# Layer 1: the last two chunks' weights summed on four column groups, with a DRAM trip of their own

## The chip, the cores and the metric

The kernel runs on one core of a Trainium2 chip. The metric is the device time of one execution in microseconds (us), lower is better. The engines are PE (matrix products), DVE (vector), ACT (scalar), POOL (GpSimd) and SP, which here only issues DMAs. Each engine takes its own instructions strictly in the order in which the program lists them.

## The reference, cut to what matters

Layer 0 is an attention block over 4096 positions with a gate; it is not touched. Layer 1 is what the change lies in:

```python
qkv = einsum('oc,bchw->bohw', w_qkv, x) + b_qkv        # b=2, 4 heads of 64, 4096 positions
attn = softmax(einsum('bhdn,bhdm->bhnm', q, k) * 64**-0.5, axis=-1)
out = einsum('bhnm,bhdm->bhdn', attn, v)
x = einsum('oc,bchw->bohw', w_out, out) + b_out + x
```

The sums of the softmax, that is the sum over m of the exponentials for each query n, are what the changed lines compute.

## The kernel before, in words

**Units and chunks.** Layer 1 works through 32 units, one for each image b, pair of heads g and block j of 512 queries. A unit goes over the 4096 keys in 32 chunks of 128, for both heads at once, so a chunk's weights are a tile `raw` of 128 keys x (2 heads x 512 queries), all in 32-bit floats. Sixteen chunks make a half n of a unit (NG = 2), and each half has its own maximum; `losts` holds the factor that puts the first half onto the second half's maximum.

**The pipeline.** One step t of the main loop handles a pair of chunks, and 16 steps make a unit. In step t the scores of pair t are made (PE, `score`, L888), their running maximum is taken (DVE, L905) and they are copied out of PSUM into the ring of raw tiles (ACT, L906, in `keep`). Eleven steps later (LAG = 11) the pair's maximum is added (DVE, `shift`, L977), the exponential is taken (ACT, `weigh`, L989), POOL adds the chunk to the sum of its half (L999 for the first two chunks of a half, L1001 for later ones), and PE multiplies it with the values (`gather`, L1030). The ring has 26 tiles, so the copy of chunk c + 26 (L906) can't start before all readers of chunk c, POOL's addition among them, are done. POOL also adds the shift to one chunk of each half itself (L966).

**Written order.** Every instruction keeps its program order on its engine (`seq`). Steps that don't belong to the pair at hand are hung on a step and a place by `at(t, place, ...)`. The places in a step are, in this order: scores, weights of an odd chunk, "start", "early", first chunk of the pair, "early end", second chunk, `gather`, "late", "late end", last shift, "end".

**The sums of a unit.** POOL doesn't add a unit's last two chunks (m = 30 and 31; L993 returns before). Instead, when `gather` reaches chunk 31 it takes the one PSUM bank of the pool `psm` (`misc`, one buffer, shared with keys, values, queries and transposes) and multiplies both chunks with a matrix of ones (L1043): four products of 32 output rows each, for two chunks and two heads, which go to PSUM rows 64 and 96. So two products write rows 64 to 95 and two write rows 96 to 127, and the second chunk is accumulated onto the first. One step later `total` (L1060) adds POOL's sums: four products for two halves and two heads, to rows 0, 32, 64 and 96; those of the second half are accumulated onto the chunks' sums. Another step later `keep_total` copies the bank to an SBUF tile `srow` (ACT, L1068; buffer "kv", two buffers, shared with the stores of keys and values), writes its four rows to DRAM (SP, L1073), reads them back turned, so that queries lie along partitions (SP, L1075), and takes the exponential for `losts`. Two steps later POOL's `add_sums` (L1151, L1152) joins the halves; then come `factors` (DVE L1158, POOL L1159) and `rows` (DVE L1169, POOL L1175 and L1178), which apply them to the outputs.

With t1 = t0 + 24 for a unit that starts at step t0, the chunks' products are at step t1 + 3 (which is step 11 of the next unit), `total` at t1 + 4, `keep_total` at t1 + 5, `add_sums` at t1 + 7. The last unit is summed in another way, so 31 units have these steps. In units 24 to 31 there is no work for later keys and values; they finish the first image's output instead, and POOL has two more additions there (L1206).

Of the kernel before, what the change touches and what calls it, by code (L numbers as in the profile page):

```python
# [8 lines left out]
F32 = mybir.dt.float32  # L9
AF = mybir.ActivationFunctionType  # L10
ALU = mybir.AluOpType
# [3 lines left out]
P = 128  # L15
NB = 512
# [4 lines left out]
D1 = 64  # L21
# [5 lines left out]
def conv_attention_kernel(  # L27
# [19 lines left out]
    nc = tc.nc  # L47
    B, _, N = x.shape
    NJ = N // NB
    NM = N // P  # L50
    PB = NB // P
# [156 lines left out]
    seq = tc.keep_in_program_order  # L208
# [3 lines left out]
    def at(t, place, step):  # L212
        extras.setdefault((t, place), []).append(step)
# [19 lines left out]
    with own0:  # L233
# [417 lines left out]
        def misc(name):  # L651
            return small_bank[0](name)
# [118 lines left out]
    with (  # L771
# [23 lines left out]
            (u, n): dram.tile([2, NB], F32, tag=f"neg_{u}_{n}", name=f"neg_{u[0]}{u[1]}{u[2]}_{n}")  # L795
            for u in units for n in range(NG)
        }
        sum1 = {
            u: dram.tile([NG * 2, NB], F32, tag="sum_{}_{}_{}".format(*u), name=f"sum_{u}")
            for u in units  # L800
        }
        first, begun, late = {}, set(), {}


# [217 lines left out]
        def gather(t):  # L1022
            u = b, g, j = units[t // NM]
            m = t % NM
            n = m // GS
            if m % GS == 0:
                avs1[u, n] = psv.tile([P, NB], F32, tag="av", name=f"av1_{b}_{g}_{j}_{n}")
            v = vs[b, g, m // PB]
            for k in range(2):
                seq(nc.tensor.matmul(  # L1030
                    avs1[u, n][k * D1 : (k + 1) * D1, :], v[:, m % PB, k, :], raws[t][:, k, :],
                    start=(m % GS == 0), stop=(m % GS == GS - 1),
                ))
            if on_tensor(t) and t % 2 == 1 and t != 2 * END - 1:
                late_sums((t - 1, t) if on_tensor(t - 1) else (None, t))
            elif t == 2 * END - 2:
                late_sums((t, t + 1))
            if m == NM - 1 and u != units[-1]:
                srows[u] = misc(f"sum1_{b}_{g}_{j}")
                for i in (t - 1, t):  # L1040
                    for k in range(2):
                        r = D1 * (NG - 1) + 32 * k
                        seq(nc.tensor.matmul(  # L1043
                            srows[u][r : r + 32, :], ones[:, :32], raws[i][:, k, :],
                            start=(i < t), stop=False, skip_group_check=True,
                        ))
            raws.pop(t - 2, None)
            if m % GS == GS - 1:
                a = l1.tile([P, NB], F32, tag="avs", name=f"avs1_{b}_{g}_{j}_{n}")
                seq(nc.scalar.copy(a, avs1.pop((u, n))))  # L1050
                avs1[u, n] = a

        def total(u):


            b, g, j = u
            for n in range(NG):
                for k in range(2):
                    r = D1 * n + 32 * k
                    seq(nc.tensor.matmul(  # L1060
                        srows[u][r : r + 32, :], ones[:, :32], accs[u, n][:, k, :],
                        start=(n < NG - 1), stop=True, skip_group_check=True,
                    ))

        def keep_total(u):
            b, g, j = u
            row = l1.tile([P, NB], F32, tag="kv", name=f"srow_{b}_{g}_{j}")
            seq(nc.scalar.copy(  # L1068
                row.rearrange("p (a m i) -> p a i m", m=P, i=2),
                srows[u].rearrange("p (a i m) -> p a i m", m=P, i=2),  # L1070
            ))
            for m in range(2 * NG):
                nc.sync.dma_start(out=sum1[u][m : m + 1, :], in_=row[32 * m : 32 * m + 1, :])  # L1073
            s = small.tile([P, NG, 2, PB], F32, tag="sums1", name=f"sums1_{b}_{g}_{j}")
            nc.sync.dma_start(  # L1075
                out=s.rearrange("p n k (a i) -> p (n k a) i", i=2),
                in_=sum1[u].rearrange("m (a p i) -> p (m a) i", p=P, i=2),
            )
            srows[u] = s
            seq(nc.scalar.activation(losts[u], losts[u], AF.Exp, scale=D1**-0.5))  # L1080

        def turned(a, name):
# [66 lines left out]
        def add_sums(u):  # L1149
            s, lost = srows[u], losts[u]  # L1150
            seq(nc.gpsimd.tensor_tensor(s[:, 0], s[:, 0], lost, ALU.mult))  # L1151
            seq(nc.gpsimd.tensor_tensor(s[:, 1], s[:, 1], s[:, 0], ALU.add))  # L1152

        def factors(u):
# [69 lines left out]
        for n, u in enumerate(units):  # L1224
            b, g, j = u
            t0 = n * US
            if n > 0:
                at(t0 - 9, "start", lambda u=u, b=b, j=j: fetch(("q", u), x1[b][j]))
                for q in range(4):
                    at(t0 - (3, 3, 2, 2)[q], "late", lambda u=u, q=q: next_queries(u, q))  # L1230
                at(t0 - 2, "start", lambda u=u: keep_next_queries(u, 0))
                at(t0 - 1, "start", lambda u=u: keep_next_queries(u, 1))
            if n < len(units) - NJ:
                to = (*units[n + NJ][:2], j)
                at(max(t0 - 1, 0), "start", lambda to=to: fetch(("kv", *to), x1[to[0]][to[2]]))
                for q in range(4):
                    at(t0 + 2 + q, "late", lambda to=to, q=q: next_keys(*to, q))
                    at(t0 + (6, 7, 9, 10)[q], "late", lambda to=to, q=q: next_values(*to, q))
                at(t0 + 6, "start", lambda to=to: store_keys(*to))
                for i, step in enumerate((t0 + 8, t0 + 11)):  # L1240
                    at(step, "start", lambda to=to, i=i: store_values(*to, i))

                t1 = (n // NJ * NJ + NJ - 1) * US
                at(t1 + 2 * j + 2, "start", lambda to=to: load_keys(*to))
                at(t1 + 2 * j + 3 + LAG, "start", lambda to=to: load_values(*to))
            for k in range(NG):
                t1 = t0 + (k + 1) * GS // 2
                places = ("early", "early" if (u, k) == (units[-1], NG - 1) else "late")
                for i, place in enumerate(places):
                    at(t1, place, lambda u=u, k=k, i=i: turn_max(u, k, i))  # L1250
                    at(t1, f"{place} end", lambda u=u, k=k, i=i: fold(u, k, i))
                at(t1 + 2, "end", lambda u=u, k=k: place_shift(u, k))
            t1 = t0 + US + GS // 2
            if u != units[-1]:
                at(t1 + 4, "late", lambda u=u: total(u))
                at(t1 + 5, "start", lambda u=u: keep_total(u))
                at(t1 + 1, "late", lambda u=u: lose(u))
                at(t1 + 7, "late end", lambda u=u: add_sums(u))
                at(t1 + 8, "end", lambda u=u: factors(u))
                for place, k in (("early", 1), ("late", 0)):  # L1260
                    at(t1 + 9, place, lambda u=u, k=k: turn_sums(u, k))
                    at(t1 + 9, f"{place} end", lambda u=u, k=k: rows(u, k))
            else:
                at(END + 1, "late", lambda u=u: last_lost(u))
                at(END + 4, "early", lambda u=u: late_sums((None, None)))
                at(END + 4, "early end", lambda u=u: keep_late(0))
                at(END + 5, "early", lambda u=u: turn_late(0))
                at(END + 5, "early end", lambda u=u: add_late(u, 0))
                at(END + 6, "early", lambda u=u: turn_sums(u, 0))
                at(END + 6, "early end", lambda u=u: first_rows(u))  # L1270
                at(END + LAG, "late", lambda u=u: turn_late(1))
                at(END + LAG, "late", lambda u=u: add_late(u, 1))
                at(END + LAG, "late", lambda u=u: turn_sums(u, 1))
                at(END + LAG, "late", lambda u=u: last_rows(u))
            if n >= len(units) - NJ:
                b0 = B - 2
                at(t0 - 1, "start", lambda b0=b0, j=j: fetch_output(b0, j))
                for o in range(CC):
                    for q in range(4):
                        step = t0 + ((2, 3, 4, 5), (6, 7, 9, 10))[o][q]  # L1280
                        at(step, "late", lambda b0=b0, j=j, o=o, q=q: project_out(b0, j, o, q))
                at(t0 + 6, "start", lambda b0=b0, j=j: output(b0, j, 0, 2))
                for part, step in enumerate((t0 + 8, t0 + 11)):
                    at(step, "start", lambda b0=b0, j=j, part=part: output(b0, j, 1, part))
# [172 lines left out]
```

## Time and profile before

| | |
|---|---|
| median of 3 runs | 4640.9 us (4640.56 to 4641.03) |
| the profiled execution's own time | 4640.95 us |
| its span, first to last instruction | 4639.2 us |
| layer 1, first scores | at 2057.8 us |
| one unit of layer 1 | 78.9 us (79.0 in the last eight) |
| mean granted TensorE clock | 0.996 |

The profile is of one execution. A row of a group of instructions reads: line of the kernel, engine, operation, result<-operands, how many; then busy time in all and the mean of one in ns; then idle time of the engine just before them and what ended most of it. A row of the timeline reads: start in us from the span's start, length in us, engine, line, operation; in brackets the engine's idle time before it and what ended it. A suffix "xN" in the timeline means that N instructions that followed closely are merged. Every fp32 matmul is recorded as two instructions. PEld is PE's loading of weights, which overlaps its products.

### The profile page before, as it was taken

How to read it: one execution, taken by the hardware profiler on the slowest of the kernel's cores; microseconds unless marked ns; L12 is line 12 of the kernel's file. 1: busy time of each engine (PE TensorE's matmuls, PEld its weight loads, DVE VectorE, ACT ScalarE, POOL GpSimd, SP SyncE). 2: the span in 40 equal slices, each digit the busy share in tenths (PEclk: the TensorE clock that was granted, in tenths of full speed). 3: DMA queues.
4: the chain of work that ended last, by engine and by line, in shares of the span. 5: the costliest groups of instructions: out<-in, count | busy, mean ns of one | idle time of the engine just before them, and what ended most of it. 6: DMA issues, size and time to landing. Idle time of an engine off the chain costs nothing. (4 is left out here: it accounts for less than half of the span.)

```text
span 4639.2 us, 73122 instructions
## 1 busy us (share of the span) xinstructions
PE 4499.0 (97%) x28490; PEld 1511.6 (33%) x28490; DVE 3833.4 (83%) x4443; ACT 3439.9 (74%) x4588; POOL 2514.8 (54%) x1307
## 2 busy tenths in 40 slices
PE   8999999999999999999999999999999999999998
PEld 3433333333333333333333333333333333323332
DVE  6777777777777777529999999999999999999997
ACT  3266666666666666668888888888888888888885
POOL 5300000000000000008999999999999999999995
PEclk9999999999999999999999999999999999999999
DMA  3100000000000000121111221111211112111213
GB/s 101 39 4 20 20 20 15 15 15 15 15 15 15 15 13 13 33 75 40 35 42 35 55 56 39 37 40 42 71 42 36 39 33 62 51 53 37 53 40 112
DMA packets 190475, 174.84 MB, mean 38 GB/s; under 512 B 120232, under 2 KB 121064, under 8 KB 190128
## 3 DMA queue, kind: packets, MB, share of 16 engines
q1 hardware_dynamic: 188272, 169.58, 13.2%
q8 instruction: 223, 3.65, 0.3%
q14 instruction: 124, 1.02, 0.1%
q10 hardware_dynamic: 1856, 0.59, 0.1%
HBM read 127.65 MB, written 42.48 MB: 37 GB/s over the span
## 5 line engine op out<-in xcount | busy, mean ns | idle before, releaser
L1001 POOL TENSOR_TENSOR acc<-acc,raw 128x1024 f32<-128x1024 f32 x821 | 1950.4, 2376 | 80.1 <-ACT raw L989 30.7
L402 DVE TENSOR_REDUCE mx<-a 128x1 f32<-128x512 f32 x2048 | 1315.5, 686 | 449.9 <-PE a L398 448.8
L439 ACT ACTIVATE p<-s 128x512 f32<-128x512 f32 x2048 | 1108.3, 595 | 702.5 <-PE a L398 367.6
L905 DVE TENSOR_TENSOR rmax<-s,rmax 128x1024 f32<-128x1024 f32 x960 | 1171.6, 1220 | 99.7 <-PE s L888 89.6
L436 PE MATMUL s<-q,kT 32*128 32x512 f32 x4096 | 1218.8, 640 | 0.0
L888 PE MATMUL s<-q,k 64*128 64x512 f32 x4096 | 1120.3, 637 | 98.1 <-ACT raw L906 93.2
L906 ACT COPY raw<-s 128x1024 f32<-128x1024 f32 x1024 | 1035.6, 1011 | 240.8 <-DVE rmax L905 163.5
L977 DVE TENSOR_TENSOR raw<-raw,shift 128x1024 f32<-128x1024 f32 x961 | 1160.7, 1212 | 3.3 <-ACT shift L959 1.8
L989 ACT ACTIVATE raw<-raw 128x1024 f32<-128x1024 f32 x1024 | 1084.9, 1060 | 62.8 <-DVE raw L977 27.7
L398 PE MATMUL a<-kT,q 32*128 32x512 f32 x4096 | 1129.8, 643 | 1.4 <-DVE mx L402 1.3
L1030 PE MATMUL av<-raw,v 128*64 128x512 f32 x4096 | 1007.4, 607 | 4.2 <-ACT raw L989 2.5
L451 PE MATMUL av<-p,v 128*32 128x256 f32 (+1 forms) x7904 | 650.1, 399 | 0.6 <-ACT avs L465 0.6
L501 POOL TENSOR_TENSOR f<-f,dyn 128x16 f32<-128x16 f32 x15 | 3.3, 221 | 1028.2 <-DVE f L500 1028.2
L888 PEld LDWEIGHTS s<-q,k 64*128 64x128 f32 x4096 | 316.8, 185 | 678.7 <-ACT raw L906 487.0
L436 PEld LDWEIGHTS s<-q,kT 32*128 32x128 f32 x4096 | 397.7, 183 | 426.3 <-issue 392.1
L1030 PEld LDWEIGHTS av<-raw,v 128*64 128x64 f32 x4096 | 242.4, 136 | 650.8 <-issue 476.4
L451 PEld LDWEIGHTS av<-p,v 128*32 128x32 f32 x7904 | 157.7, 108 | 751.5 <-issue 737.3
L552 POOL TENSOR_SCALAR res<-res 128x1024 f32<-128x1024 f32 x16 | 16.7, 1044 | 660.3 <-ACT res L551 660.3
L398 PEld LDWEIGHTS a<-kT,q 32*128 32x128 f32 x4096 | 305.2, 184 | 31.4 <-DVE mx L402 18.2
L999 POOL TENSOR_TENSOR acc<-raw,raw 128x1024 f32<-128x1024 f32 x64 | 152.1, 2376 | 60.9 <-ACT raw L989 60.3
L966 POOL TENSOR_TENSOR raw<-raw,row 128x1024 f32<-128x1024 f32 x63 | 151.7, 2407 | 37.9 <-DMA row<-neg 37.9
L935 DVE TENSOR_REDUCE negs<-rt 128x4 f32<-128x512 f32 x126 | 87.0, 690 | 58.8 <-PE rt L918 58.8
(338 smaller groups left out, 1913.5 us busy)
## 6 DMA issues: line engine op xcount, KB each, us to landing
row<-neg SPq DMA_DIRECT2D x64, 512.0 KB
x<-in_x_dram SPq DMA_DIRECT2D x16, 512.0 KB
res<-in_x_dram SPq DMA_DIRECT2D x16, 512.0 KB
x<-res SPq DMA_DIRECT2D x16, 512.0 KB
att<-rows SPq DMA_DIRECT2D x62, 128.0 KB
kd<-k1s SPq DMA_DIRECT2D x24, 256.0 KB
vd<-v1s SPq DMA_DIRECT2D x24, 256.0 KB
k<-kd SPq DMA_DIRECT2D x24, 256.0 KB
```

The costliest lines, as they stand in the source:

```text
L398: seq(nc.tensor.matmul(ps, qs0[u][r, bass.ts(i, P)], kTs[b][r, bass.ts(m, NB)], start=True, stop=True,))
L402: seq(nc.vector.tensor_reduce(mxs[u][:, i * H + h, m : m + 1], ps, AX.X, ALU.max))
L436: seq(nc.tensor.matmul(ps, kTs[b][r, bass.ts(m, P)], qs0[u][r, :], start=True, stop=True))
L439: seq(nc.scalar.activation(pt[:, k, :], ps, AF.Exp, scale=D0**-0.5))
L451: seq(nc.tensor.matmul(avs[u][32 * h : 32 * h + 32, cols], vs0[b][:, m, 32 * h : 32 * h + 32], pts[t, h // 2][:, h % 2, cols], start=(m == ...
L888: seq(nc.tensor.matmul(ps[:, k, :], ks[b, g, m // PB][r, bass.ts(m % PB, P)], qs1[u][r, :], start=True, stop=True,))
L905: seq(nc.vector.tensor_tensor(rmax[u, n], ps, before, ALU.max))
L906: seq(nc.scalar.copy(raw, ps))
L977: seq(nc.vector.tensor_tensor(raws[t], raws[t], shifts[u, t % NM // GS], ALU.add))
L989: seq(nc.scalar.activation(p, p, AF.Exp, scale=D1**-0.5))
L1001: seq(nc.gpsimd.tensor_tensor(accs[u, n], accs[u, n], p, ALU.add))
L1030: seq(nc.tensor.matmul(avs1[u, n][k * D1 : (k + 1) * D1, :], v[:, m % PB, k, :], raws[t][:, k, :], start=(m % GS == 0), stop=(m % GS == GS ...
```

## The change

The two last chunks' sums no longer share a PSUM bank with `total`. In `gather`, the four products write four different groups of 32 rows (32 columns of the PE array each) of a bank `csums`: rows 0 and 32 for chunk 30, rows 64 and 96 for chunk 31, nothing accumulated. A new step `keep_chunks`, hung on (t1 + 4, "start"), copies that bank to an SBUF tile (ACT), writes four rows to DRAM and reads them back turned (five DMAs on SP); `keep_total` does the same for `total` as before, through the common function `keep_rows`. `total` takes the `misc` bank anew and writes it with four products that accumulate nothing. `add_sums` adds the chunks' sums with two more additions of 128x8 on POOL.

```diff
             if m == NM - 1 and u != units[-1]:
-                srows[u] = misc(f"sum1_{b}_{g}_{j}")
-                for i in (t - 1, t):
+
+                csums[u] = misc(f"csum1_{b}_{g}_{j}")
+                for i in range(2):
                     for k in range(2):
-                        r = D1 * (NG - 1) + 32 * k
+                        r = D1 * i + 32 * k
                         seq(nc.tensor.matmul(
-                            srows[u][r : r + 32, :], ones[:, :32], raws[i][:, k, :],
-                            start=(i < t), stop=False, skip_group_check=True,
+                            csums[u][r : r + 32, :], ones[:, :32], raws[t - 1 + i][:, k, :],
+                            start=True, stop=True,
                         ))
...
             b, g, j = u
+            srows[u] = misc(f"sum1_{b}_{g}_{j}")
             for n in range(NG):
                 for k in range(2):
                     r = D1 * n + 32 * k
                     seq(nc.tensor.matmul(
                         srows[u][r : r + 32, :], ones[:, :32], accs[u, n][:, k, :],
-                        start=(n < NG - 1), stop=True, skip_group_check=True,
+                        start=True, stop=True,
                     ))
 
-        def keep_total(u):
-            b, g, j = u
-            row = l1.tile([P, NB], F32, tag="kv", name=f"srow_{b}_{g}_{j}")
+        def keep_rows(ps, to, tag, name):
+
+            row = l1.tile([P, NB], F32, tag="kv", name=f"srow_{name}")
             seq(nc.scalar.copy(
                 row.rearrange("p (a m i) -> p a i m", m=P, i=2),
-                srows[u].rearrange("p (a i m) -> p a i m", m=P, i=2),
+                ps.rearrange("p (a i m) -> p a i m", m=P, i=2),
             ))
-            for m in range(2 * NG):
-                nc.sync.dma_start(out=sum1[u][m : m + 1, :], in_=row[32 * m : 32 * m + 1, :])
-            s = small.tile([P, NG, 2, PB], F32, tag="sums1", name=f"sums1_{b}_{g}_{j}")
+            for m in range(4):
+                nc.sync.dma_start(out=to[m : m + 1, :], in_=row[32 * m : 32 * m + 1, :])
+            s = small.tile([P, 2, 2, PB], F32, tag=tag, name=f"sums1_{name}")
             nc.sync.dma_start(
                 out=s.rearrange("p n k (a i) -> p (n k a) i", i=2),
-                in_=sum1[u].rearrange("m (a p i) -> p (m a) i", p=P, i=2),
+                in_=to.rearrange("m (a p i) -> p (m a) i", p=P, i=2),
             )
-            srows[u] = s
+            return s
+
+        def keep_chunks(u):
+            csums[u] = keep_rows(csums[u], csum1[u], "csums", "c_{}_{}_{}".format(*u))
+
+        def keep_total(u):
+            srows[u] = keep_rows(srows[u], sum1[u], "sums1", "{}_{}_{}".format(*u))
             seq(nc.scalar.activation(losts[u], losts[u], AF.Exp, scale=D1**-0.5))
...
             seq(nc.gpsimd.tensor_tensor(s[:, 0], s[:, 0], lost, ALU.mult))
+            c = csums.pop(u)
+            seq(nc.gpsimd.tensor_tensor(s[:, 0], s[:, 0], c[:, 0], ALU.add))
+            seq(nc.gpsimd.tensor_tensor(s[:, 1], s[:, 1], c[:, 1], ALU.add))
             seq(nc.gpsimd.tensor_tensor(s[:, 1], s[:, 1], s[:, 0], ALU.add))
...
             if u != units[-1]:
+                at(t1 + 4, "start", lambda u=u: keep_chunks(u))
                 at(t1 + 4, "late", lambda u=u: total(u))
                 at(t1 + 5, "start", lambda u=u: keep_total(u))
```

More of the change, by code (lines that the diff above doesn't have):

```diff
@@ L797, in conv_attention_kernel @@
         }
[L798 to L801, printed above, removed]
+        sum1, csum1 = (
+            {
+                u: dram.tile([4, NB], F32, tag="{}_{}_{}_{}".format(s, *u), name=f"{s}_{u}")
+                for u in units
+            }
+            for s in ("sum", "csum")
+        )
+        csums = {}
         first, begun, late = {}, set(), {}
```

## The prediction

> **What bounds the kernel now.** I read the page first.
>
> ```profile
> PE 4499.0 (97%) x28490; PEld 1511.6 (33%) x28490; DVE 3833.4 (83%) x4443; ACT 3439.9 (74%) x4588; POOL 2514.8 (54%) x1307
> ```
>
> These shares mix two layers. By stage, 2620 to 3020 us in layer 1 has PE busy 384 of 400 us, DVE 375, ACT 354, POOL 376: three engines are nearly full, and POOL is one of them, with its 2.38 us additions. So I then asked the groups of layer 1 (from 2150 us on) what the change's products cost:
>
> ```profile
> L1043 PE MATMUL sum<-raw,ones 128*32 128x512 f32 x248 | 59.2, 598 | 0.0
> ...
> L1060 PE MATMUL sum<-acc,ones 128*32 128x512 f32 x248 | 33.0, 605 | 0.0
> ```
>
> The same number of products of the same shape takes 59.2 us where two share a row group and 33.0 us where four have one each. Third, the timeline of one boundary (the sums of unit 13; all boundaries repeat it at 78.9 us):
>
> ```profile
> 3202.48 1.91 PE L1043 MATMUL sum<-raw,ones 128*32 128x512 f32 x8
> ...
> 3204.32 1.99 PE L888 MATMUL s<-q,k 64*128 64x512 f32 x8
> ...
> 3205.50 1.22 DVE L905 TENSOR_TENSOR rmax<-s,rmax 128x1024 f32<-128x1024 f32 x1 [1.55 <-PE s L888]
> ...
> 3206.81 1.01 ACT L906 COPY raw<-s 128x1024 f32<-128x1024 f32 x1 [0.92 <-DVE rmax L905]
> ```
>
> DVE stands 1.55 us for scores that stand behind L1043, so at this point PE is the late one. POOL alone, same stretch:
>
> ```profile
> 3205.97 2.37 POOL L999 TENSOR_TENSOR acc<-raw,raw 128x1024 f32<-128x1024 f32 x1 [2.26 <-ACT raw L989]
> 3209.09 17.09 POOL L1001 TENSOR_TENSOR acc<-acc,raw 128x1024 f32<-128x1024 f32 x7 [0.75 <-ACT raw L989]
> 3226.14 0.20 POOL L1151 TENSOR_TENSOR sums<-sums,lost 128x8 f32<-128x8 f32 x1
> 3226.41 0.20 POOL L1152 TENSOR_TENSOR sums<-sums 128x8 f32<-128x8 f32 x1
> 3226.57 4.83 POOL L1001 TENSOR_TENSOR acc<-acc,raw 128x1024 f32<-128x1024 f32 x2
> ```
>
> These two waits are POOL's only idle time in a unit: seven additions in 17.09 us are 2.44 us each, two per step are 4.9 us, while a plain step lasts 4.52 us (four DVE operations at 1.13 us). POOL falls behind all along the half. Who waits for it is seen at the end of that half, 40 us later in each unit. Here it is for unit 11's chunks:
>
> ```profile
> 3009.52 2.41 POOL L1001 TENSOR_TENSOR acc<-acc,raw 128x1024 f32<-128x1024 f32 x1
> ...
> 3010.42 1.22 DVE L905 TENSOR_TENSOR rmax<-s,rmax 128x1024 f32<-128x1024 f32 x1
> ...
> 3011.97 1.01 ACT L906 COPY raw<-s 128x1024 f32<-128x1024 f32 x1 [0.38 <-POOL acc L1001]
> ```
>
> The copy of chunk 41 (chunk 9 of the next unit) needs the ring tile of chunk 15, whose addition POOL ends here, and the maximum of its own chunk. Normally such a copy starts 0.09 us after the maximum ends. In unit 11 it started 0.03 us after POOL's end (3011.93) and 0.33 us after the maximum (3011.64): POOL held it. In the other units both end together: in unit 13 POOL at 3169.51, the maximum at 3169.54, and the copy starts at 3169.63. Over the units the median is 0.09 us after POOL's end, so POOL has some 0.055 us to spare here. The next closest is chunk 16, which L999 frees 2.4 us later, with 0.17 us to spare; after that 0.6 us and more.
>
> **What the Trainium skill says.** TensorEngine Tiling, Key Properties: different tiles can execute in parallel; the trace agrees (1.91 and 1.06 us per unit for eight recorded products). Its PSUM Bottleneck section adds that the copy out of PSUM is not made faster; here it is even doubled. PSUM — Partial Sum Buffer, Engine vs sequencer instructions: the queues of ScalarE, VectorE and GpSimd are strict FIFO; the trace agrees, POOL's small additions stand between the large ones. GPSIMD Engine Reference, Elementwise side-by-side: about 156 ns of dispatch for an instruction, listed for DVE, with two software hops on GpSimd; the trace has 0.16 us from the start of an independent 128x8 addition to the next (3226.41 to 3226.57) and 0.27 us where the next depends on it.
>
> **The change, part by part.**
>
> *PE.* L1043 to the next scores is 1.84 us (3202.48 to 3204.32), L1060 to the next 0.99 us (3208.11 to 3209.10). The new form gains 0.85 us per unit. Can the scores use it? Their two banks are free at 3202.58 and 3204.45 (ends of L906), so the first pair starts at 3203.47, the second at 3204.5, and DVE's maximum moves from 3205.50 to 3204.65: all of it. This alone is 31 x 0.85 = 26.3 us.
>
> *ACT.* One more copy, 0.63 us long as L1068's (31 of them, 19.5 us), 0.53 us from its start to the next start. It comes after the exponential L989 of 3204.80, so at 3205.77; the next L906 starts at 3206.30, before at 3206.81. ACT had 0.92 us idle there, which hides it. Without that cover it would cost 31 x 0.53 = 16.4 us. The next exponential, for POOL's second addition, starts at 3207.2 in place of 3207.88.
>
> *PE behind the bank.* `total` now waits until the copy has emptied the one `misc` bank, at 3206.4; PE gets there at 3208.10 - 0.85 = 3207.3. Scores queue behind it; 0.9 us to spare, cost nothing.
>
> *SP and DMA.* Four writes (0.28 us each to issue) and a read (0.38) go ahead of `keep_total`'s five. SP is idle from 3202.0 to 3211.8, and a trip takes 3.9 us from first issue to last packet (3211.8 to 3215.7): from 3206.4 it ends near 3210.3, before the other trip starts and 15 us before POOL needs it. `srow` now takes the buffer of the values' store; that one was issued at 3201.70 and its last packet ended at 3203.4, the copy comes at 3210.3. Nothing.
>
> *POOL.* Two more 128x8 additions in `add_sums`. One hangs on the operation before it, one is independent: 0.28 + 0.16 = 0.44 us. The bounds: L1159, placed between two large additions, costs only 0.04 us over the usual 2.446, so two cost 0.09 at least; if both pay a dependence and a wait they cost 0.6. Neither can be under nothing, since the queue only grows. I take 0.44.
>
> *Where it lies.* POOL's first addition at a boundary hangs on an ACT queue that is full since 3199.3 and gains nothing. Its second starts at 3208.42 in place of 3209.09, when the first has ended: 0.67 us earlier. From there to chunk 15 POOL has no gap, and the two additions take 0.44 back: 0.23 us earlier, 0.28 with the 0.055 spare. The other engines want to be 0.85 earlier, so the copy of chunk 41 is held 0.57 us. What follows absorbs some: DVE has 0.02 us at the maximum after the next scores and 0.12 up to 3179.91, PE 0.18 at 3175.37, so 0.14 us. (In unit 11 the hold was 0.25, and from its sums back to the unit before's it was 79.0 us for 78.9: 0.25 - 0.14 = 0.11.) Gain per unit 0.28 + 0.14 = 0.42, or in general 0.87 - x for POOL's x.
>
> The last eight units are tighter, POOL having two more additions:
>
> ```profile
> 4072.78 1.26 POOL L1206 TENSOR_TENSOR xo_('xo', 0, 1)_31483<-xo_('xo', 0, 1)_31483,y 128x512 f32<-128x512 f32 x1
> 4074.17 2.37 POOL L999 TENSOR_TENSOR acc<-raw,raw 128x1024 f32<-128x1024 f32 x1
> 4077.21 4.84 POOL L1001 TENSOR_TENSOR acc<-acc,raw 128x1024 f32<-128x1024 f32 x2 [0.67 <-ACT raw L989]
> ```
>
> POOL's own idle time is 0.16 + 0.58 = 0.74 us a unit (a gap of 0.08 is usual), so the gain is at most 0.74 - 0.44 = 0.30. In the last unit POOL waits again by itself (4.85 us at 4576), so the last boundary keeps some 0.8.
>
> *Sum.* 22 x 0.42 + 8 x 0.30 + 0.8 = 12.4 us. The profiled execution took 4640.95 us (span 4639.2 and 1.75 around it), 0.05 from the median: 4640.95 - 12.4 = 4628.5.
>
> **The rivals.** *PE alone counts*, POOL's additions fall into gaps or have spare that I don't see: 4640.95 - 26.3 = 4614.7. For it: POOL is recorded roughly, and L1159 costs 0.04. Against it: the 0.03 us of unit 11. *The gain is not passed on*: PE's four products don't overlap as L1060's, or ACT's copy lands late and moves POOL's second addition back; then the gain per unit is 0 to 0.25: 4641 to 4633, taken as 4637. *POOL becomes the bound*: one mechanism, at `add_sums`, its price x. The new additions wait for a semaphore of the DMA besides POOL's own, which no addition of L1151's size shows together. From x = 0.87 (0.74 in the last eight units) the change costs time; with x = 1.3 it is 22 x 0.43 + 8 x 0.56 - 0.8 = 13.1 us slower, 4654. It takes 0.65 us for each small addition, more than double what L1151 shows. That the change doesn't do what it says is unlikely: the listing has the same PE order, one more copy, two more additions per unit.
>
> **How the numbers follow.** Held by POOL as worked out: 0.62; with x from 0.6 to 0.09 this is 22 x 0.27 + 8 x 0.14 + 0.8 = 7.9 to 22 x 0.78 + 8 x 0.65 + 0.8 = 23.2 us, so 4633 to 4618. PE alone 0.12, not passed on 0.15, POOL the bound 0.11. Some 0.2% (9.3 us) is what a measurement of this kernel can tell from no change. Faster by more: below 4631.7, three quarters or more of the first case and all of the second, 0.60. Within: the rest of the first, nearly all of the third, 0.29. Slower: 0.11. The range goes from the second case to the middle of the third and a bit on: 4614 to 4641.
>
> **What would show it.** The new products take 1.06 us per unit; DVE's wait at the boundary falls from 1.55 to about 0.7; POOL's second wait of 0.75 us goes; four small POOL additions start within 0.88 us; L906 waits for POOL some 0.4 us longer once in a unit, 40 us after the sums; the unit lasts 78.5 us. I'd be wrong if units last 78.05 (POOL has spare), if ACT's new copy starts after its neighbours and L906 is not earlier, or if the small additions take over 0.4 us each.

## The result and the profile after

The changed kernel takes 4629.06 us (median of 11 runs, 4627.19 to 4629.80) where the kernel before takes 4640.64 us on the same chip (11 runs): a ratio of 0.9975, 95% interval 0.9966 to 0.9983. It is 11.6 us faster; the forecast was 12.4 us (4628.5).

The profiled execution's span is 4627.1 us, 12.1 less than before. First a line of the page, then the group of the new products in layer 1 from 2150 us on (busy us, then mean ns of one). Line numbers have moved: L1043 is now L1048, L1060 is L1066, L1068 is L1074, L888 is L892, L906 is L910, L989 is L993, L999 and L1001 are L1003 and L1005.

```profile
PE 4467.1 (97%) x28490; PEld 1502.0 (32%) x28490; DVE 3835.3 (83%) x4443; ACT 3452.5 (75%) x4619; POOL 2527.5 (55%) x1369
```

```profile
L1048 PE MATMUL csum<-raw,ones 128*32 128x512 f32 x248 | 33.0, 605 | 0.0
```

The products do what the change says: 59.2 us have become 33.0, 0.85 us a unit. The span fell by less than half of these 26.2 us, while PE's share stayed at 97%; the share doesn't show the loss, the places where engines wait for each other do. This is the timeline of the boundary after the same unit as before:

```profile
3197.39 1.07 PE L1048 MATMUL csum<-raw,ones 128*32 128x512 f32 x8
...
3198.35 1.01 ACT L910 COPY raw<-s 128x1024 f32<-128x1024 f32 x1
...
3198.39 2.15 PE L892 MATMUL s<-q,k 64*128 64x512 f32 x8
...
3199.41 0.30 PEld L892 LDWEIGHTS s<-q,k 64*128 64x128 f32 x4 [0.72 <-ACT raw L910]
3199.56 1.23 DVE L909 TENSOR_TENSOR rmax<-s,rmax 128x1024 f32<-128x1024 f32 x1 [0.71 <-PE s L892]
3199.72 1.08 ACT L993 ACTIVATE raw<-raw 128x1024 f32<-128x1024 f32 x1
...
3200.47 1.94 PE L1034 MATMUL av<-raw,v 128*64 128x512 f32 x8
3200.68 0.65 ACT L1074 COPY srow_c<-csum 128x512 f32<-128x512 f32 x1
...
3201.19 1.03 ACT L910 COPY raw<-s 128x1024 f32<-128x1024 f32 x1
```

DVE's wait has fallen from 1.55 to 0.71 us, and ACT's new copy stands where ACT was idle for 0.92 us. POOL alone, same stretch:

```profile
3200.88 2.39 POOL L1003 TENSOR_TENSOR acc<-raw,raw 128x1024 f32<-128x1024 f32 x1 [2.02 <-ACT raw L993]
3203.35 17.10 POOL L1005 TENSOR_TENSOR acc<-acc,raw 128x1024 f32<-128x1024 f32 x7
3220.40 0.20 POOL L1163 TENSOR_TENSOR sums<-sums,lost 128x8 f32<-128x8 f32 x1
3220.68 0.21 POOL L1165 TENSOR_TENSOR sums<-sums,sums_c 128x8 f32<-128x8 f32 x1
3220.85 0.20 POOL L1166 TENSOR_TENSOR sums<-sums,sums_c 128x8 f32<-128x8 f32 x1
3221.13 0.20 POOL L1167 TENSOR_TENSOR sums<-sums 128x8 f32<-128x8 f32 x1
3221.29 4.82 POOL L1005 TENSOR_TENSOR acc<-acc,raw 128x1024 f32<-128x1024 f32 x2
```

The second wait (0.75 us before) is gone: the second addition starts 2.47 us after the first, where it was 3.12; the small operations take 0.89 us from the first's start to the next large addition, where two took 0.43. And this is where POOL ends chunk 15 of unit 13 and the copy of chunk 41 starts:

```profile
3162.26 2.39 POOL L1005 TENSOR_TENSOR acc<-acc,raw 128x1024 f32<-128x1024 f32 x1
...
3162.95 1.22 DVE L909 TENSOR_TENSOR rmax<-s,rmax 128x1024 f32<-128x1024 f32 x1
...
3164.69 1.01 ACT L910 COPY raw<-s 128x1024 f32<-128x1024 f32 x1 [0.56 <-POOL acc L1005]
```

The maximum ends at 3164.17, so without POOL the copy would start 0.09 us later, at 3164.26; POOL ends at 3164.65, and the copy starts 0.04 us after that. By how much the copy starts later than 0.09 us after its maximum is called its hold below. In the trace of before four of the 30 units were held here by 0.05 us or more; now each is, with 0.44 us as the median hold.

From POOL's first addition in one unit to that in the next (L999, L1003) it is on average 78.91 us before and 78.49 after in the first 22, 79.04 and 78.77 in the last eight. Together: 22 x 0.414 + 8 x 0.277 = 11.3 us; what follows the last boundary gives 1.1 more, and the stretch ahead of the first boundary was 0.4 longer in this execution: together the 12.1 us of the span, to the rounding.

### The profile page after: what moved, and what is told of

Same layout as the page of the kernel before. It is cut to its first block, busy times and chain, and to the rows that moved or that the text cites. A ratio compares the mean times of both kernels' runs of the same rounds, so it can differ in the third digit from the quotient of the medians.

```text
span 4627.1 us, 73487 instructions
## 1 busy us (share of the span) xinstructions
PE 4467.1 (97%) x28490; PEld 1502.0 (32%) x28490; DVE 3835.3 (83%) x4443; ACT 3452.5 (75%) x4619; POOL 2527.5 (55%) x1369
## 5 line engine op out<-in xcount | busy, mean ns | idle before, releaser
L1005 POOL TENSOR_TENSOR acc<-acc,raw 128x1024 f32<-128x1024 f32 x821 | 1951.2, 2377 | 59.2 <-ACT raw L993 7.7
L892 PE MATMUL s<-q,k 64*128 64x512 f32 x4096 | 1114.0, 635 | 119.3 <-ACT raw L910 114.3
L910 ACT COPY raw<-s 128x1024 f32<-128x1024 f32 x1024 | 1038.3, 1014 | 219.7 <-DVE rmax L909 146.2
L993 ACT ACTIVATE raw<-raw 128x1024 f32<-128x1024 f32 x1024 | 1088.4, 1063 | 60.9 <-DVE raw L981 27.6
L892 PEld LDWEIGHTS s<-q,k 64*128 64x128 f32 x4096 | 313.7, 185 | 696.7 <-ACT raw L910 547.0
L1003 POOL TENSOR_TENSOR acc<-raw,raw 128x1024 f32<-128x1024 f32 x64 | 152.7, 2386 | 54.8 <-ACT raw L993 54.8
```

The lines of the kernel that those rows point to most:

```text
L892: seq(nc.tensor.matmul(ps[:, k, :], ks[b, g, m // PB][r, bass.ts(m % PB, P)], qs1[u][r, :], start=True, stop=True,))
L910: seq(nc.scalar.copy(raw, ps))
L993: seq(nc.scalar.activation(p, p, AF.Exp, scale=D1**-0.5))
L1005: seq(nc.gpsimd.tensor_tensor(accs[u, n], accs[u, n], p, ALU.add))
```

## The experiments

The theory to be tested: POOL's chain of additions, which frees the ring's tiles, takes the place of PE as what sets a unit, so that the gain is 0.87 us minus x, x being the price of the added work on POOL, and no more than PE's own gain. Each variant was timed against the kernel before on the same chip, but not all on one chip: compare the ratios, not the times. "Unit" is the distance of POOL's first additions, in the first 22 units and in the last eight. In the diffs, "..." stands for lines left out; before_*, and pe_alone, are edits of the kernel before, the others of the changed kernel.

| kernel | us | before, us | ratio, 95% interval | unit, us |
|---|---|---|---|---|
| kernel before | 4640.64 | | | 78.91, 79.04 |
| changed kernel | 4629.06 | 4640.64 | 0.9975, 0.9966 to 0.9983 | 78.49, 78.77 |
| before_two_adds | 4645.83 | 4639.17 | 1.0014, 1.0008 to 1.0021 | 79.11, 79.24 |
| after_no_adds | 4620.23 | 4639.17 | 0.9959, 0.9947 to 0.9972 | 78.22, 78.44 |
| after_four_adds | 4636.40 | 4639.17 | 0.9994, 0.9986 to 1.0003 | 78.79, 79.04 |
| after_spread | 4619.61 | 4639.17 | 0.9957, 0.9945 to 0.9970 | 78.22, 78.42 |
| pe_alone | 4618.42 | 4638.89 | 0.9956, 0.9942 to 0.9970 | 78.20, 78.42 |
| trip_two_groups | 4646.57 | 4638.89 | 1.0017, 1.0010 to 1.0024 | 79.13, 79.29 |
| after_ring27 | 4621.00 | 4638.89 | 0.9962, 0.9950 to 0.9975 | 78.22, 78.75 |
| before_ring27 | 4640.13 | 4638.89 | 1.0004, 0.9996 to 1.0013 | 78.89, 79.16 |
| spread_early | 4620.21 | 4640.18 | 0.9959, 0.9945 to 0.9972 | 78.19, 78.29 |
| before_early | 4646.69 | 4640.18 | 1.0014, 1.0008 to 1.0021 | 79.03, 79.17 |
| before_spread | 4640.16 | 4640.18 | 1.0000, 0.9992 to 1.0008 | 78.89, 79.03 |

**before_two_adds: POOL's price without the rest.**

```diff
...
             seq(nc.gpsimd.tensor_tensor(s[:, 0], s[:, 0], lost, ALU.mult))
+            seq(nc.gpsimd.tensor_tensor(s[:, 0], s[:, 0], zeros[:, 0], ALU.add))
+            seq(nc.gpsimd.tensor_tensor(s[:, 1], s[:, 1], zeros[:, 1], ALU.add))
             seq(nc.gpsimd.tensor_tensor(s[:, 1], s[:, 1], s[:, 0], ALU.add))
```

> The kernel before, with two more small additions on GpSimd at the place where the changed kernel has its two; they add a tile of zeros, so the sums stay the same. Nothing else of the change is in it. Theory (GpSimd's chain of additions, through the ring of raw tiles, sets the length of a unit as soon as it is delayed): the additions cost 0.44 us of GpSimd time, of which 0.055 is spare and 0.14 is absorbed later, so a unit takes 0.25 us longer, 30 x 0.25 = 7.5 us, some 4648 us, and the copy of chunk 41 waits for GpSimd in every unit. Rival (TensorE alone sets the unit, GpSimd has room): no change, 4640.6 us.

Measured: 6.7 us slower for an expected 7.5, 0.21 us a unit. In this kernel's timeline the copy of chunk 41 (here L908) is held:

```profile
3090.11 2.40 POOL L1003 TENSOR_TENSOR acc<-acc,raw 128x1024 f32<-128x1024 f32 x1
...
3090.84 1.22 DVE L907 TENSOR_TENSOR rmax<-s,rmax 128x1024 f32<-128x1024 f32 x1
...
3092.55 1.01 ACT L908 COPY raw<-s 128x1024 f32<-128x1024 f32 x1 [0.53 <-POOL acc L1003]
```

The copy starts 0.04 us after POOL's end (3092.51) and 0.49 after the maximum's (3092.06). Two additions of 0.2 us on an engine that is busy 54% of the whole time lengthen the kernel. The rival, that PE alone sets the unit, falls. The median hold over the units is 0.38 us for 0.21 of lengthening, so some 0.17 was absorbed, not 0.14.

**after_no_adds, after_four_adds: the price to nothing, and up.**

```diff
-            c = csums.pop(u)
-            seq(nc.gpsimd.tensor_tensor(s[:, 0], s[:, 0], c[:, 0], ALU.add))
-            seq(nc.gpsimd.tensor_tensor(s[:, 1], s[:, 1], c[:, 1], ALU.add))
+            csums.pop(u)
```

> The changed kernel without the two added GpSimd additions: the sums of a unit's last two chunks are made, copied and taken through DRAM, but not added, so the softmax lacks these two chunks' weights in its sums. Theory: GpSimd's price goes to nothing and TensorE's 0.85 us a unit comes through, in the last eight units some 0.70; 22 x 0.85 + 8 x 0.70 + 0.8 = 25 us, 4616 us. Rival (the rest of TensorE's gain went to ScalarE's copy and the trip through DRAM): the time stays at about 4629 us.

Measured: 18.9 us faster than before, 4620.2 for an expected 4616. The hold is gone (median 0.00), and a unit of the first 22 gains 0.69 us, not 0.85. So the additions cost 0.69 - 0.41 = 0.28 us a unit, and something else caps the gain at 0.69.

```diff
...
             seq(nc.gpsimd.tensor_tensor(s[:, 1], s[:, 1], c[:, 1], ALU.add))
+            seq(nc.gpsimd.tensor_tensor(s[:, 0], s[:, 0], zeros[:, 0], ALU.add))
+            seq(nc.gpsimd.tensor_tensor(s[:, 1], s[:, 1], zeros[:, 1], ALU.add))
             seq(nc.gpsimd.tensor_tensor(s[:, 1], s[:, 1], s[:, 0], ALU.add))
```

> The changed kernel with two further additions of zeros on GpSimd beside its two. Theory: GpSimd's price is 0.88 us a unit in place of 0.44, the gain of 0.87 minus that price is gone, in the last eight units it is a loss of 0.2: 4641 to 4642 us, and a unit takes 78.9 us. Rival (the time is not set by GpSimd): 4629 us as the changed kernel.

Measured: 4636.4 us for an expected 4641 to 4642; 0.12 us a unit is still gained, where none was expected. The direction is the theory's; the size is a slip of mine about x, the price of the additions, as POOL's timeline shows (starts of L1167, L1168, L1169, L1170):

```profile
3223.41 0.20 POOL L1167 TENSOR_TENSOR sums<-sums,sums_c 128x8 f32<-128x8 f32 x1
3223.57 0.20 POOL L1168 TENSOR_TENSOR sums<-sums,sums_c 128x8 f32<-128x8 f32 x1
3223.73 0.20 POOL L1169 TENSOR_TENSOR sums<-sums,zeros 128x8 f32<-128x8 f32 x1
3223.89 0.20 POOL L1170 TENSOR_TENSOR sums<-sums,zeros 128x8 f32<-128x8 f32 x1
```

L1169 needs L1167, but L1168 stands between, so its start is 0.16 us after the last and not 0.28. From the start of POOL's second addition of a unit to the end of chunk 15 it is 39.35 us before, 39.80 in the changed kernel and 40.10 here: x is 0.45, and 0.75 here. 0.87 - 0.75 = 0.12 is what was measured, and 0.87 - 0.45 = 0.42 is the changed kernel's 0.41.

**after_spread: the same sums, placed otherwise.**

```diff
...
+                at(t1 + 6, "late end", lambda u=u: scale_sums(u))   # s[:, 0] *= lost
+                at(t1 + 7, "start", lambda u=u: add_chunks(u))      # s += c, 16 columns
                 at(t1 + 7, "late end", lambda u=u: add_sums(u))     # s[:, 1] += s[:, 0]
```

> The changed kernel with the joining of the sums done by three GpSimd operations (scale the first half; add both chunks' sums in one operation of 16 columns; join the halves), each set between two large additions of their own instead of one after the other. Theory: a small operation set alone between two large ones costs 0.04 us, since it fills the gap of 0.08 that a dependent large addition leaves; three cost 0.12 where the kernel before paid 0.32 for two, so GpSimd ends earlier than before and TensorE's 0.85 us comes through in all units: 4614 to 4616 us. Rival (only the number of operations counts, three in place of two): 0.16 to 0.28 us a unit stay on GpSimd, 4620 to 4624 us.

Measured: 4619.6 us, 19.6 faster than before, though 4614 to 4616 was expected. No kernel that makes the reference's sums is faster. POOL's timeline shows why it gains on the changed kernel:

```profile
3207.93 2.37 POOL L1005 TENSOR_TENSOR acc<-acc,raw 128x1024 f32<-128x1024 f32 x1
3210.26 0.21 POOL L1163 TENSOR_TENSOR sums<-sums,lost 128x8 f32<-128x8 f32 x1
3210.41 2.38 POOL L1005 TENSOR_TENSOR acc<-acc,raw 128x1024 f32<-128x1024 f32 x1
3212.76 0.21 POOL L1167 TENSOR_TENSOR sums<-sums,sums_c 128x16 f32<-128x16 f32 x1
3212.93 2.37 POOL L1005 TENSOR_TENSOR acc<-acc,raw 128x1024 f32<-128x1024 f32 x1
```

From one large addition to the next it is 2.48 and 2.52 us with a small operation between, 2.44 to 2.45 without. The same stretch to chunk 15 is 39.16 us, 0.19 less than before. The rival (numbers of operations alone) expected 4620 to 4624 and its time isn't excluded, but it needs 0.16 to 0.28 us more on POOL than before, and POOL's rows show 0.19 less. The hold is 0.00, and again a unit of the first 22 gains 0.69.

**before_spread: POOL's relief without PE's gain.** The same with the two operations of the kernel before (scale at t1 + 6, join at t1 + 7).

> The kernel before with its two joining operations on GpSimd set one half step apart, each alone between two large additions, nothing else. GpSimd has 0.24 us less per unit. Theory: before the change TensorE sets the unit, GpSimd's release is not late: no change, 4639 us. Rival (GpSimd set the unit all along): 30 x 0.24 = 7 us faster, 4632 us.

Measured: no change (0.9992 to 1.0008), though POOL's stretch is 0.25 us shorter (39.10). Before the change POOL was second, not first. And the two operations are the same here, so the 0.25 comes from placing alone, which the rival of after_spread leaves out.

**pe_alone and trip_two_groups: the two halves of the change apart.**

```diff
-                for i in (t - 1, t):
+                for i in range(2):
                     for k in range(2):
-                        r = D1 * (NG - 1) + 32 * k
+                        r = D1 * i + 32 * k
                         seq(nc.tensor.matmul(
-                            srows[u][r : r + 32, :], ones[:, :32], raws[i][:, k, :],
-                            start=(i < t), stop=False, skip_group_check=True,
+                            srows[u][r : r + 32, :], ones[:, :32], raws[t - 1 + i][:, k, :],
+                            start=True, stop=False, skip_group_check=True,
...
-                        start=(n < NG - 1), stop=True, skip_group_check=True,
+                        start=False, stop=True, skip_group_check=True,
```

> The kernel before with only the four products of the last two chunks spread over four row groups of the one bank, on which the sums of the halves are then accumulated; no second bank, copy, trip or addition. Chunk 30 lands in the first half's sum and so gets the first half's factor: the softmax sums are not the reference's. Theory: the same as the changed kernel without its two additions, 4616 us, since the copy and the trip are hidden. Rival (the copy and the trip cost): this one is clearly faster than that one, by up to 31 x 0.53 = 16 us if the copy is not hidden at all.

```diff
-                        r = D1 * i + 32 * k
+                        r = D1 + 32 * k
                         seq(nc.tensor.matmul(
                             csums[u][r : r + 32, :], ones[:, :32], raws[t - 1 + i][:, k, :],
-                            start=True, stop=True,
+                            start=(i == 0), stop=(i == 1), skip_group_check=True,
                         ))
...
```

> The changed kernel with the two last chunks' products on two row groups again (the second chunk accumulated onto the first, as in the kernel before), but with the bank, the copy, the trip and two GpSimd additions of its own (one of them adds zeros). Theory: without TensorE's gain only GpSimd's price is left, 0.25 us a unit as in the kernel before with two more additions: 4648 us. Rival (the copy and the trip cost as well): up to 31 x 0.53 = 16 us more, 4664 us; rival (the extra work is free): 4640.6 us.

Measured: pe_alone is 20.5 us faster than before (0.70 us a unit). It falls short of the expected gain as after_no_adds does, which on its chip gained 18.9. Their units differ by 0.02 us, and their two intervals overlap: of the 16 us that an unhidden copy would cost, the copy and the trip take 1.6 by these medians, so they are all but hidden. trip_two_groups is 7.7 us slower than before (7.4 was expected), and its unit of 79.13 is that of before_two_adds (79.11): of the work that the change adds, the two additions are what costs.

**after_ring27, before_ring27: the link itself.**

```diff
-        tc.tile_pool(name="ring", bufs=2 * LAG + 4) as ring,
+        tc.tile_pool(name="ring", bufs=2 * LAG + 5) as ring,
...
-        def fetch(key, src, tag="xb", bufs=3, pool=l1x):
+        def fetch(key, src, tag="xb", bufs=2, pool=l1x):
...
```

> The changed kernel with 27 raw tiles in the ring in place of 26 (room made by two input buffers in place of three, and the third of the last inputs in a ring tile). Theory (the hold works through the ring's release of chunk 15): the copy of chunk 41 now waits for chunk 14, which is done 2.4 us earlier; the hold goes and TensorE's 0.85 us comes through in the first 22 units, in the last eight, where GpSimd has no idle time left, 0.23 stay: 22 x 0.85 + 8 x 0.23 + 0.8 = 21 us, 4619 us. Rival (GpSimd delays something else, or the loss is elsewhere): 4629 us.

> The kernel before with the same 27 raw tiles and the same buffers. Theory: before the change TensorE sets the unit, and GpSimd's release comes 0.055 us early, so the tile brings nothing: 4640.6 us, a unit of 78.9 us. Rival (GpSimd already set the unit before): faster by several us.

Measured: with one more tile and POOL's work unchanged (39.78 us to chunk 15), the hold is gone and the changed kernel takes 4621.0 us for an expected 4619; a unit is 78.22 in the first 22, as with no additions at all. The copy of chunk 41 no longer waits for the addition of chunk 15, which ends 0.37 us after the copy's start:

```profile
3158.43 2.38 POOL L1005 TENSOR_TENSOR acc<-acc,raw 128x1024 f32<-128x1024 f32 x1
...
3160.44 1.01 ACT L910 COPY raw<-s 128x1024 f32<-128x1024 f32 x1
```

In the last eight, where POOL has no idle time to catch up in, it is 78.75, as in the changed kernel. The kernel before doesn't gain (4640.1; its first 22 units 78.89). So the delay reaches the others through the ring, and in the last eight units through POOL's own load.

**spread_early, before_early: what caps the gain at 0.69.**

```diff
-                    at(t0 + (6, 7, 9, 10)[q], "late", lambda to=to, q=q: next_values(*to, q))
+                    at(t0 + (6, 7, 9, 9)[q], "late", lambda to=to, q=q: next_values(*to, q))
...
-                for i, step in enumerate((t0 + 8, t0 + 11)):
+                for i, step in enumerate((t0 + 8, t0 + 10)):
                     at(step, "start", lambda to=to, i=i: store_values(*to, i))
...
```

> The changed kernel with the three joining operations spread, and besides with the last quarter of the next values (in the last eight units, of the output) one step earlier, so that ScalarE's copy of them (0.35 us) stands one step ahead of the boundary and not in it. The runs so far say that without GpSimd's hold a unit gains 0.69 us and not 0.85. Theory for the missing 0.16: at the boundary the second pair of scores waits for its PSUM bank, which ScalarE's copy frees late, since the copy of the values stands ahead of it; then this run gains the 0.16 and ScalarE's own earlier start: 31 x 0.16 = 5 us or more, 4614 us or less. Rival (another place sets the 0.69): 4619.6 us as without the move, or slower, since TensorE's step before is fuller.

> The kernel before with the same quarter and copy one step earlier, nothing else. Theory: before the change TensorE's two groups set the boundary and the bank is free when it ends, so the move brings nothing: 4639 us. Rival (the move helps by itself): as much faster as the changed kernel is with it.

Measured: spread_early isn't faster than after_spread (4620.2, where 4614 or less was expected), so as an improvement the move fails: it makes PE's step before the boundary fuller, and by itself costs 6.5 us (before_early), where no change was expected. But against before_early, which has the same fuller step, spread_early takes 26.5 us less, and its unit is 79.03 - 78.19 = 0.84 us shorter: with the copy of the values out of the way, PE's whole 0.85 comes through. This takes it that the fuller step costs both kernels the same, which no run tests. Rows of spread_early at the boundary:

```profile
3195.78 1.00 ACT L910 COPY raw<-s 128x1024 f32<-128x1024 f32 x1
...
3196.09 1.99 PE L892 MATMUL s<-q,k 64*128 64x512 f32 x8
...
3198.01 1.94 PE L1034 MATMUL av<-raw,v 128*64 128x512 f32 x8
```

From the scores' start to the next products it is 1.92 us, as in the kernel before (3204.32 to 3206.24); in the changed kernel it is 2.08 (3198.39 to 3200.47). There the second pair of scores stands for its bank, which the copy L910 of 3198.35 frees at 3199.36, and the load of its weights stands with it (PEld at 3199.41): the pair starts 1.02 us after the first in place of 0.96, and its recorded products then come in two steps 0.53 us apart in place of 0.43. That is the missing 0.16. In the last eight units the same stretch takes 2.18 us in place of 1.92, and there the kernels without the two additions gain 0.60 to 0.62 us a unit, near 0.85 - 0.26.

## Why the prediction was right

**PE.** Right in the price of the products (1.06 us, as forecast) and in DVE's wait, which falls by 0.84 us; wrong in "all of it". The prediction saw that the second pair of scores has its bank only at 3204.45, a shade late, but charged nothing for it: PE gains 0.69 us to the rest of the unit. The term mis-sized is the 0.85, by 0.16. It did no harm to the sum, since POOL let only 0.41 through. It does harm to the rival "PE alone counts", whose 4614.7 should have been some 4619, and to the upper end of the first case: 23.2 us at x = 0.09 can't be had when after_no_adds, with x = 0, gains 18.9.

**ACT, the bank, SP and DMA.** Right. The next copy comes 0.51 us after the new one for 0.53; `total` isn't held; pe_alone and after_no_adds show nothing worth naming for copy and trip.

**POOL.** Right in place, way and size. x is 0.45 for 0.44. Counted from the boundary, the addition of chunk 15 ends 0.21 us earlier (0.23 was forecast) and the copy of chunk 41 starts 0.26 earlier (0.28, medians both); the rest of a unit's gain, 0.15 for a forecast of 0.14, is absorbed later: 0.41 for 0.42. The hold is 0.44 us and not 0.57: 0.69 - 0.26 is 0.43, so that is the same mis-sized term again. The lines of the last eight units show POOL without a wait, as the prediction had it:

```profile
4063.66 1.28 POOL L1221 TENSOR_TENSOR xo_('xo', 0, 1)_31777<-xo_('xo', 0, 1)_31777,y 128x512 f32<-128x512 f32 x1
4064.90 2.40 POOL L1003 TENSOR_TENSOR acc<-raw,raw 128x1024 f32<-128x1024 f32 x1
4067.38 4.84 POOL L1005 TENSOR_TENSOR acc<-acc,raw 128x1024 f32<-128x1024 f32 x2
```

They gain 0.28 for 0.30. Together the units gain 11.3 us for 11.6; after the last boundary 1.1 us came for 0.8. That these two make up for each other is luck, of a third of a microsecond.

**The rivals.** "PE alone counts" falls with before_two_adds, after_ring27 and after_no_adds. "The gain is not passed on": partly true, by 0.16 us, for another reason than it gave. "POOL becomes the bound" has the right mechanism, but its price is not met: after_four_adds puts 0.75 us on POOL, below the 0.87 from which that case begins, and is still not slower.

The 20 us that the cap of 0.69 allows are had by after_spread. What removing the cap without filling another step would add, 0.16 x 31 = 5 us, is an estimate; no run reached it.

## What to carry to other kernels

An engine that is full for a while and then waits can hold the others in the middle and look idle on average: follow its lag to the place where a buffer of a ring is given back, and take the spare there, not the idle time, as what added work may use. Where a change speeds up one engine, ask which other loop is next and how much it has in hand; here POOL had some 0.2 us in hand, so of 0.45 us of small additions 0.28 a unit came through, 8 of the 20 us that the change could bring. On a queue that is the bound, try setting small operations singly between large ones; here that gave the 8 us back.

## What the runs showed of the hardware that was not expected

A 128x8 POOL operation that is recorded with 0.20 us costs 0.04 to 0.08 us when it stands alone between two large additions that depend on each other (after_spread), 0.16 to 0.17 where the next operation doesn't need its result, and 0.28 where the next needs it (after, after_four_adds). A pair of scores that starts 0.06 us late for its bank makes PE's next products 0.16 us late; the load of its weights is seen to wait too. Four fp32 products of 32 output rows side by side take 1.06 us, two side by side 0.96 (half of 1.91): the four cost a tenth more than the two.
